# Cross-attention on one core: the fourth batch's x loaded one slot earlier, two query copies and the last products reordered, the first normalisation cut in halves

## The chip, the cores and the metric

The kernel runs on one core of a Trainium2 chip. A core has five engines with queues of their own: TensorE (PE, matmuls; PEld is its weight load), VectorE (DVE), ScalarE (ACT), GpSimd (POOL) and SyncE (SP), which here issues nearly all DMAs. Each engine takes its instructions in the order of the program, and they wait for each other by semaphores. The metric is the device time of one execution in microseconds: the median of several runs. Beside it stands one execution with the hardware profiler on.

## The reference

Eight batches of 256 tokens with 1024 columns attend to 256 context rows; 32 heads of 32 columns; everything is float32.

```python
residual = hidden_states                       # x, (8, 256, 1024)
x = (hidden_states - mu) * rsqrt(var + 1e-5) * ln_gamma + ln_beta
Q = _split_heads(x @ Wq.T)
K = _split_heads(memory_keys)                  # both are the context
V = _split_heads(memory_values)
scores = einsum('bhsd,bhtd->bhst', Q, K) * HEAD_DIM ** (-0.5)
scores = where(mask, scores, -inf)
probs = softmax(scores, axis=-1)
attn = einsum('bhst,bhtd->bhsd', probs, V)     # then heads side by side
return residual + attn @ Wout.T
```

## The kernel before

**Slots.** The work is cut into `N` = 64 slots, `n`, eight to a batch (`NQ` = 8). A slot stands for four heads (128 columns) of one batch. The loop at L903 writes the whole program out by hand; no scheduler reorders it. In slot `n` TensorE computes the scores of `n + 1` (`scores`, L471), the product of probabilities and values of `n - 2` (`values`, L614), query columns of later slots (`make_q`, L331, and from batch 3 `query_product`, L432), and a share of the output projection of the batch before (`product_steps`, L681). Queries and projection of most batches are done as 7 products of half-size blocks instead of 8, with sums of the weights and of the operands (names S1 to S4, T1 to T4, A11 to A22, B11 to B22); POOL makes these sums.

**Softmax.** `softmax_parts` (L491) of slot `n + 1` runs in slot `n`. For each of four heads: VectorE subtracts and takes a minimum (L515), ScalarE takes the exponential with its sum (L519), VectorE the reciprocal (L526), POOL scales (`normalize`, L528), and VectorE transposes in blocks of 32 (`blocks`, L534) into the tile `pT`. ScalarE copies half of it to `pc` (`aside`, L540). Two pairs of DMAs then exchange quarters between partitions: `pT<-pT` (L600) and, after the loads of the list `between`, `pT<-pc` (L604). Those four and `between` are the function `tail`; for softmaxes 1 to 7 it is kept back and run inside the next softmax, after its first head. Softmax 8 and most later ones run theirs at once.

**The places of the query copies.** ScalarE copies query products out of PSUM (`copy_q`, L344). In `softmax_parts` the list `copies` is run after the last exponential where `n <= NQ` (L572), and else after the third block transpose (L591), behind the first `aside`. Here `n` is the number of the softmax, one more than the slot.

**PSUM.** Four banks hold scores, two the values, one (`ps_q`, tile `pq`) queries, and one (`ps_o`) both the output products `po` and, in slots 1 to 8, a second query product: `make_q(..., second=True)`. In slot 8 this second product is finished and has to be copied before slot 9 starts the first output product (A11) in the same bank. `keep_p1` (L700) copies A11 out on ScalarE after six exponentials, before the product A12 goes on in that bank.

**x.** `load_x` (L125) brings a row block of 128 tokens (512 KB). Two tiles serve x and its transposed form `xe` in turn. For each batch a table gives the slots in which the two rows are loaded, their statistics taken (`ln_stats`, L216, on VectorE), normalised (`ln_norm`, L241), transposed (`blocks_x`, L307, VectorE) and moved by DMA (`move_x`, L327, `xnT<-xe`). For batch 3 (`SPLIT`) the rows are loaded in slots 6 and 7 (L801), and their statistics are taken in slots 8 and 9. In slots up to 8 the statistics are fillers (`fill`) between the steps of the softmax.

**Loads between.** The list `between` of slot `n` (L906 to L931) holds, in this order, keys or values, residual rows, x, mask and a table of output-weight halves (`load_wo`, L169, 512 KB each; L921). Batch 0's first residual row is loaded in slot 6 (L926).

**Start and end.** Before the loop batch 0's two rows are normalised on VectorE by one instruction each over 1024 columns (L853, L860), then transposed on TensorE; 32 transposes of the identity (L120) keep TensorE working before. After the loop the last batch's products are written out by hand (L1025 to L1084): `end_sum` makes the sums of one column block, `end_steps` adds products into PSUM, `end_add` adds PSUM to the residual. In the last slot ScalarE first runs the list `now`, a copy of a `po` bank to `ends` (`copy_po`, L707), then `copy_at` (L629), which copies the values to the tile `at`.

Of the kernel before, what the change touches and what calls it, by code (L numbers as in the profile page):

```python
# [59 lines left out]
def xattn_kernel(  # L60
# [11 lines left out]
    nc = tc.nc  # L72
    B, S, D = x.shape
# [3 lines left out]
    NQ = NC  # L77
# [9 lines left out]
    N = B * NQ  # L87
# [150 lines left out]
        else:  # L238
            later.append(pow_)

    def ln_norm(b, s, engine):  # L241
        if engine is nc.scalar:
            shift = sm.tile([P, 1], F32, tag="shift", name=f"shift_{b}_{s}", bufs=2)
            nc.gpsimd.tensor_scalar(
                shift, mvs[b][:, s, 0:1], rstds[b][:, s : s + 1], -1.0, ALU.mult, ALU.mult
            )
            engine.activation(
                xs[b][:, s, :], xs[b][:, s, :], AF.Identity,
                bias=shift, scale=rstds[b][:, s : s + 1],
            )  # L250
            return
        engine.tensor_scalar(
            xs[b][:, s, :], xs[b][:, s, :], mvs[b][:, s, 0:1], rstds[b][:, s : s + 1],
            ALU.subtract, ALU.mult,
        )

# [234 lines left out]
    def softmax_parts(n, copies=(), ahead=(), between=(), hooks={}, fill=()):  # L491

        fill = list(fill)

        def fill_in():
            if fill:  # L500
                fill.pop(0)()

        pss = scs[n]
        pT = pTs[n] = ptp.tile([P, 2, NI, NH, NS, K], F32, tag="pT", name=f"pT_{n}")
        pc = asp.tile([P, NI, NH, NS, K], F32, tag="pc", name=f"pc_{n}")
        es, mns, dens = {}, {}, {}

        def exps(j, part=range(NS)):
            if 0 in part:
                es[j] = ep.tile([P, NS, T], F32, tag="e", name=f"e_{n}_{j}")  # L510
                mns[j] = sm.tile([P, NS], F32, tag="mn", name=f"mn_{n}_{j}")
                dens[j] = sm.tile([P, NS], F32, tag="den", name=f"den_{n}_{j}")
            e, mn, den = es[j], mns[j], dens[j]
            for s in part:
                nc.vector.tensor_tensor_reduce(  # L515
                    out=e[:, s, :], in0=pss[j][:, s, :], in1=mbs[n // NQ], scale=1.0,
                    scalar=NO_SCORE, op0=ALU.add, op1=ALU.min, accum_out=mn[:, s : s + 1],
                )
                nc.scalar.activation(  # L519
                    e[:, s, :], e[:, s, :], AF.Exp, bias=mn[:, s : s + 1], scale=-1.0,  # L520
                    accum_out=den[:, s : s + 1],
                )

        def normalize(j):
            rden = sm.tile([P, NS], F32, tag="rden", name=f"rden_{n}_{j}")
            nc.vector.reciprocal(rden, dens[j])  # L526
            for s in range(NS):
                nc.gpsimd.tensor_scalar(  # L528
                    es[j][:, s, :], es[j][:, s, :], rden[:, s : s + 1], 1.0,
                    ALU.mult, ALU.mult,  # L530
                )

        def blocks(j):
            nc.vector.transpose(  # L534
                pT[:, :, :, j, :, :].rearrange("p a i s k -> p (a i) s k"),
                es[j].rearrange("p s (b t) -> p b s t", t=K),
            )

        def aside(j):
            nc.scalar.copy(pc[:, :, ts(j, 2)], pT[:, 1, :, ts(j, 2)])  # L540

        if n == 0:
            for j in range(NH - 1):
                exps(j, (0,))
            yield
            exps(NH - 1, (0,))
            fill_in()
            yield
            for j in range(NH):
                exps(j, (1,))  # L550
            normalize(0)
            fill_in()
        else:
            exps(0)
            while tails:
                tails.pop()()
            late = "p1" in hooks
            if not late:
                for done in list(pvs):
                    copy_at(done)  # L560
            exps(1)
            for hook in hooks.get("soon", ()):
                hook()
            exps(2)
            normalize(0)
            for hook in hooks.get("p1", ()):
                hook()
            exps(3)
            if late:
                for done in list(pvs):  # L570
                    copy_at(done)
        if n <= NQ:  # L572
            for copy in copies:
                copy()
        for hook in hooks.get(0, ()):
            hook()
        normalize(1)
        fill_in()
        blocks(0)
        for hook in hooks.get(1, ()):  # L580
            hook()
        normalize(2)
        fill_in()
        blocks(1)
        aside(0)
        normalize(3)
        fill_in()
        blocks(2)
        while fill:
            fill_in()  # L590
        if n > NQ:  # L591
            for copy in copies:
                copy()

        def tail():
            blocks(3)
            aside(1)

            for r in range(2):
                nc.sync.dma_start(pT[ts(2 * r, K), 1], pT[ts(2 * r + 1, K), 0])  # L600
            for load in between:
                load()
            for r in range(2):
                nc.sync.dma_start(pT[ts(2 * r + 1, K), 0], pc[ts(2 * r, K)])  # L604

        for load in ahead:
            load()
        if n < NQ or N - NQ < n < N - 1:
            tails.append(tail)
        else:  # L610
            tail()
        yield
# [145 lines left out]
    def end_steps(po, name, which, chunks, begins=(), cols=slice(0, 512)):  # L758

        for c in chunks:  # L760
            nc.tensor.matmul(  # L761
                po, end_operand(name)[:, c], wo[:, which, c, cols],
                start=c in begins, stop=True, skip_group_check=True,
            )
# [25 lines left out]
    for b in range(1, B):  # L790
        first = NQ * (b - 1) + 2
        if b == 1:
            when = dict(moves=())
        elif b == 2:
            when = dict(
                loads=(0, 1), stats=(2, 3), norms=(3, 3), trans=(4, 5),
                moves=tuple(5 + (i + 2) // 6 for i in range(16)),
            )
        else:
            when = dict(  # L800
                loads=(first - 12, first - 11) if b == SPLIT else (first - 13, first - 12),  # L801
                stats=(first - 10, first - 9) if b == SPLIT else (first - 11, first - 9),
                norms=(first - 8, first - 7), trans=(first - 7, first - 6),
                moves=tuple(first - 6 + (i + 2) // 6 for i in range(16)),
            )
        for table, key in (
            (loads, "loads"), (stats, "stats"), (norms, "norms"), (trans, "trans"),
        ):
            for i, n in enumerate(when.get(key, ())):
                assert n < first  # L810
                table[n].append((b, i))
        for n in range(N):
            part = [i for i, slot in enumerate(when["moves"]) if slot == n]
            if part:
                assert n < first - 1
                moves[n].append((b, part))
        biases[NQ * b - 2].append(b)
        if b % 2 == 0:
            masks[NQ * b - 7].append(b)
# [30 lines left out]

    ln_stats(0, 0)
    ln_stats(0, 1, (0,))
    ln_norm(0, 0, nc.vector)  # L853
    ln_stats(0, 1, (1, 2))
    transpose_x0(0)
    early, late = (0, 1, 5, 2, 6, 3), (7, 4)
    for c in early + late:
        copy_x0(0, c, nc.vector if c > 4 else nc.scalar)
    nc.gpsimd.tensor_copy(xnT0[:, :, S], bet)
    ln_norm(0, 1, nc.vector)  # L860
    first_q(0, early + late)
    mask_bias(0)
    transpose_x0(1)
# [39 lines left out]
    for n in range(N):  # L903
# [15 lines left out]
        between += [partial(load_x, *args) for args in loads[n]]  # L919
        between += [partial(load_mask, one) for one in masks[n]]  # L920
        for which, pair in {  # L921
            0: ((B12, 0),), 1: ((B22, 0),), 2: ((B11, 0), (B12, 1)), 3: ((B22, 1),),
            4: ((B11, 1), (B21, 0)), 5: ((B21, 1),),
        }.get(n, ()):
            between.append(partial(load_wo, which, pair))
        if n == NQ - 2:  # L926
            between.append(partial(load_res, 0, 0, 0))
        if n == N - 4:
            again = xp.tile([P, NS, D], F32, tag="x", name="x_again")
# [22 lines left out]
        if n in products:  # L952
            query_product(*products[n])
            copies.append(partial(copy_product, *products[n]))
        for one in now:
            one()
        fill = []
        if n < 2:
            transpose_x1(2 * n)
# [5 lines left out]
        if n + 1 < N:  # L965
            softmax(n + 1, copies, ahead, between, hooks, fill)
        else:
            copy_at(n - 2)
            for load in between:
                load()  # L970
        if b >= 0 and i == 1:
# [70 lines left out]
    )  # L1042
    end_steps(to_c11, "A12", B21, (0,), (0,))
    end_steps(to_c21, "A22", T4, (0,), (0,))
    end_steps(to_c22, "S1", T1, (0,), (0,))
    end_steps(to_c11, "A12", B21, (1,))
    end_steps(to_c21, "A22", T4, (1,))
    values(N - 2)
# [8 lines left out]
    copy_at(N - 1)  # L1057
    end_sum(slice(3, 4), nc.vector)
    first_cols, last_cols = slice(0, 384), slice(384, 512)
    end_steps(to_c22, "S1", T1, (1,))  # L1060
    end_steps(s2t2, "S2", T2, (2,))
    for r in (r01, r10, r11):
        end_add(r, s2t2)
# [61 lines left out]
```

## Time and profile before

| What | us |
|---|---|
| Median of 3 runs | 577.23 (575.44 to 579.26) |
| The profiled execution, device time | 577.06 |
| Its span, first to last instruction | 575.3 |
| TensorE busy | 567.5 (99%) |
| VectorE busy | 459.1 (80%) |
| ScalarE busy | 411.6 (72%) |
| GpSimd busy | 403.8 (70%) |
| DMA queue of SyncE, share of 16 engines | 68.8% |
| Bytes moved by DMA | 117.98 MB |

A busy TensorE is not TensorE at its peak: matmuls are pipelined and their ends are modelled. The mean granted clock was 0.997 of full speed. Times in timelines count from the start of the span. In a timeline row the columns are start, duration, engine, line, operation, tiles (out<-in), shapes, count, and in brackets the idle time of that engine before the row with what ended it. In a row by stretches the columns are the stretch, its length, then the busy time with the number of instructions in brackets for PE, PEld, DVE, ACT and POOL, the granted TensorE clock, the DMA share and GB/s. In a row of waits: who waited, for what, total us, times, longest.

### The profile page before, as it was taken

What the parts mean: (1) busy time and instruction counts of PE and PEld (TensorE: products, weight loads), DVE (VectorE), ACT (ScalarE), POOL (GpSimd) and SP (SyncE); (2) the same over time, 40 slices, a digit from 0 to 9 for tenths busy, and PEclk for the clock granted to TensorE, in tenths of its full rate; (3) what the DMA queues carried; (4) which work ended last, traced back from release to release, by engine and by line L of the source; (5) the groups of instructions that cost most, each with busy time, mean ns of one, the idle gap of its engine ahead of it and who ended that gap; (6) DMA issues with size and microseconds to landing.
All of it is one profiled execution on the core that took longest, in us unless ns stands there. A gap on an engine that the chain in (4) does not pass through costs nothing.

```text
span 575.3 us, 20001 instructions
## 1 busy us (share of the span) xinstructions
PE 567.5 (99%) x7162; PEld 393.2 (68%) x7162; DVE 459.1 (80%) x1696; ACT 411.6 (72%) x1424; POOL 403.8 (70%) x675
## 2 busy tenths in 40 slices
PE   8999998999999999999999999999999999999997
PEld 8778884667667777677676677667766767755444
DVE  5897986888877879889888888888877868879824
ACT  3697886677667867698667967778766876769820
POOL 1788896899896896766567675666657657448780
PEclk9999998999999999999999999999999999999999
DMA  8667877666778677877677776897568865536751
GB/s 303 233 191 234 236 223 200 203 194 187 191 235 270 202 199 194 252 227 222 182 230 230 214 204 195 241 272 203 144 182 267 241 196 138 140 107 180 205 163 74
DMA packets 47475, 117.98 MB, mean 205 GB/s; under 512 B 9104, under 2 KB 9872, under 8 KB 47376
## 3 DMA queue, kind: packets, MB, share of 16 engines
q1 hardware_dynamic: 47088, 116.69, 68.8%
q8 instruction: 57, 0.93, 0.7%
q14 instruction: 42, 0.34, 0.2%
q10 hardware_dynamic: 288, 0.01, 0.0%
HBM read 65.28 MB, written 11.53 MB: 134 GB/s over the span
## 4 chain that ended last, share of the span: by engine, by line
PE 84%; DMA 4%; POOL 4%; DVE 3%; ACT 2%; issue 1%; SPq 1%; DVEq 0%; ACTq 0%
PE po_S L694 20%; PE pq_A L440 16%; PE po_A L694 11%; PE pv L622 11%; PE sc L479 10%; PE pq L340 7%; PE pq_S L440 6%; PE po_end L761 2%; POOL e L528 2%; DMA wq<-in_wq_dram 2%; DMA x<-in_x_dram 1%; DVE e L515 1%; ACT e L519 1%; DVE pT L534 1%; PE po_last L761 1%
## 5 line engine op out<-in xcount | busy, mean ns | idle before, releaser
L528 POOL TENSOR_SCALAR e<-e,rden 128x256 f32<-128x256 f32 x512 | 235.7, 478 | 129.5 <-DVE rden L526 127.5
L519 ACT ACTIVATE e<-e,mn 128x256 f32<-128x256 f32 x512 | 254.0, 500 | 49.4 <-DVE mn L515 48.3
L534 DVE STREAM_TRANSPOSE pT<-e 128x512 f32<-128x512 f32 x256 | 180.7, 707 | 54.0 <-POOL e L528 34.8
L515 DVE CUSTOM_DVE_ANT_0 e<-sc,mb 128x256 f32<-128x256 f32 x512 | 186.0, 416 | 24.2 <-PE sc L479 23.6
L540 ACT COPY pc<-pT 128x512 f32<-128x512 f32 x128 | 79.0, 617 | 72.1 <-DVE pT L534 42.4
L519 ACT ACTIVATION_READ_ACCUMULATOR e<-e,mn 128x1 f32 x512 | 97.8, 191 | 0.0
L340 PE MATMUL pq<-xnT,wq 128*128 128x256 f32 (+1 forms) x368 | 84.1, 382 | 0.0
L340 PEld LDWEIGHTS pq<-xnT,wq 128*128 128x128 f32 x368 | 68.7, 190 | 14.3 <-issue 4.0
L479 PEld LDWEIGHTS sc<-k,qa 32*128 32x128 f32 x1024 | 46.1, 184 | 42.4 <-issue 22.0
L622 PE MATMUL pv<-pT,v 64*32 64x128 f32 x4096 | 74.5, 274 | 0.2
L622 PEld LDWEIGHTS pv<-pT,v 64*32 64x32 f32 x4096 | 57.0, 105 | 25.6 <-issue 11.6
L694 PE MATMUL po_S<-wo,at 128*128 128x512 f32 x152 | 74.3, 606 | 0.0
L479 PE MATMUL sc<-k,qa 32*128 32x256 f32 x1024 | 73.6, 400 | 0.1
L694 PE MATMUL po_A<-wo,at 128*128 128x512 f32 x128 | 62.4, 622 | 2.7 <-ACT qa L349 2.7
L694 PE MATMUL po_S<-wo,s 128*128 128x512 f32 x104 | 50.1, 605 | 0.0
L526 DVE RECIPROCAL rden<-den 128x2 f32<-128x2 f32 x256 | 37.7, 147 | 6.6 <-ACT e L519 5.3
L515 DVE DVE_READ_ACCUMULATOR2_ANT mn<- 128x1 f32 x512 | 42.7, 83 | 0.0
L694 PEld LDWEIGHTS po_A<-wo,at 128*128 128x128 f32 x128 | 23.2, 195 | 28.3 <-issue 23.2
L440 PEld LDWEIGHTS pq_A<-xnT,wq 128*128 128x128 f32 x320 | 37.3, 192 | 4.8 <-issue 4.1
L694 PEld LDWEIGHTS po_S<-wo,at 128*128 128x128 f32 x152 | 25.8, 190 | 19.8 <-issue 19.3
L440 PE MATMUL pq_A<-xnT,wq 128*128 128x128 f32 x320 | 37.3, 275 | 0.0
L635 ACT COPY at<-pv 128x128 f32<-128x128 f32 x128 | 26.1, 253 | 9.6 <-PE pv L622 9.6
(95 smaller groups left out, 605.9 us busy)
## 6 DMA issues: line engine op xcount, KB each, us to landing
v<-in_kv_dram SPq DMA_DIRECT2D x32, 512.0 KB, 4.6
pT<-pT SPq DMA_DIRECT2D x128, 128.0 KB, 2.9
pT<-pc SPq DMA_DIRECT2D x128, 128.0 KB, 4.1
ring<-kept_T SPq DMA_DIRECT2D x18, 512.0 KB, 5.3
k<-in_kv_dram SPq DMA_DIRECT2D x32, 256.0 KB, 4.2
x<-in_x_dram SPq DMA_DIRECT2D x14, 512.0 KB, 5.6
r<-in_x_dram SPq DMA_DIRECT2D x28, 256.0 KB, 4.7
out_dram<-r SPq DMA_DIRECT2D x28, 256.0 KB, 3.4
```

The source lines that it names most:

```text
L340: nc.tensor.matmul(pqs[n], wq[:, o, c, :], xnTs[b](c), start=(c == 0), stop=(c == NC - 1),)
L440: nc.tensor.matmul(pqs[b][:, o, :], w[:, c], x_[:, c], start=begins and o + c == 0, stop=c == NK - 1, skip_group_check=True,)
L479: nc.tensor.matmul(scs[n][j][:, s, :], qa[r, n % NQ, ts(s, P)], ks[n - n % 2][r, n % 2, :], start=True, stop=True,)
L515: nc.vector.tensor_tensor_reduce(out=e[:, s, :], in0=pss[j][:, s, :], in1=mbs[n // NQ], scale=1.0, scalar=NO_SCORE, op0=ALU.add, op1=ALU.m ...
L519: nc.scalar.activation(e[:, s, :], e[:, s, :], AF.Exp, bias=mn[:, s : s + 1], scale=-1.0, accum_out=den[:, s : s + 1],)
L526: nc.vector.reciprocal(rden, dens[j])
L528: nc.gpsimd.tensor_scalar(es[j][:, s, :], es[j][:, s, :], rden[:, s : s + 1], 1.0, ALU.mult, ALU.mult,)
L534: nc.vector.transpose(pT[:, :, :, j, :, :].rearrange("p a i s k -> p (a i) s k"), es[j].rearrange("p s (b t) -> p b s t", t=K),)
L540: nc.scalar.copy(pc[:, :, ts(j, 2)], pT[:, 1, :, ts(j, 2)])
L622: nc.tensor.matmul(pvs[n][r][j * HD : (j + 1) * HD], vs[n - n % 2][ts(r, 2 * K), i, ds(n % 2 * P + j * HD, HD)], pT[ts(r, 2 * K), :, i, j, ...
L635: nc.scalar.copy(ats[b, k][:, c, :, ts(r, 2), :], pv.rearrange("p a s k -> p s a k"))
L694: nc.tensor.matmul(po, operand(b, name)[:, c], wo[:, which, c], start=begins and c == 0, stop=c == NK - 1, skip_group_check=not begins,)
```

## The change

There are five edits.

1. Batch 3's rows of x are loaded in slots 5 and 6 rather than 6 and 7. The second pairs of output weights B12 and B22 move from slots 2 and 3 to slots 3 and 4, B21's pairs from 4 and 5 to 5 and 6, and the first residual row from slot 6 to slot 7.
2. In softmax 9 (slot 8) the first query copy is run after the last exponential; the second stays late. All other softmaxes keep their places.
3. Batch 0's rows are each normalised by two instructions of 512 columns.
4. In the last slot `now` runs after `copy_at` rather than before.
5. In the end the first S1 product is no longer issued after the first A12 and A22 products; it is issued with the second S1 product, after `values(N - 1)`.

No instruction is added beyond those of edit 3. Apart from one matmul, one copy in slot 8, one copy in the last slot and the loads named, every engine has its instructions in the order it had before.

```diff
-    def ln_norm(b, s, engine):
+    def ln_norm(b, s, engine, cols=slice(0, D)):
...
-            xs[b][:, s, :], xs[b][:, s, :], mvs[b][:, s, 0:1], rstds[b][:, s : s + 1],
+            xs[b][:, s, cols], xs[b][:, s, cols], mvs[b][:, s, 0:1], rstds[b][:, s : s + 1],
...
-        if n <= NQ:
-            for copy in copies:
-                copy()
+        copies = list(copies)
+        for copy in copies[: NQ if n <= NQ else 1 if n == NQ + 1 else 0]:
+            copies.remove(copy)
+            copy()
...
-        if n > NQ:
-            for copy in copies:
-                copy()
+        for copy in copies:
+            copy()
...
-                loads=(first - 12, first - 11) if b == SPLIT else (first - 13, first - 12),
+                loads=(first - 13, first - 12),
...
-    ln_norm(0, 0, nc.vector)
+    for h in range(2):
+        ln_norm(0, 0, nc.vector, ts(h, 512))
...
-    ln_norm(0, 1, nc.vector)
+    for h in range(2):
+        ln_norm(0, 1, nc.vector, ts(h, 512))
...
-            0: ((B12, 0),), 1: ((B22, 0),), 2: ((B11, 0), (B12, 1)), 3: ((B22, 1),),
-            4: ((B11, 1), (B21, 0)), 5: ((B21, 1),),
+            0: ((B12, 0),), 1: ((B22, 0),), 2: ((B11, 0),), 3: ((B12, 1),),
+            4: ((B22, 1), (B11, 1)), 5: ((B21, 0),), 6: ((B21, 1),),
...
-        if n == NQ - 2:
+        if n == NQ - 1:
             between.append(partial(load_res, 0, 0, 0))
...
-        for one in now:
-            one()
+        if n + 1 < N:
+            for one in now:
+                one()
...
             copy_at(n - 2)
+            for one in now:
+                one()
...
-    end_steps(to_c22, "S1", T1, (0,), (0,))
...
-    end_steps(to_c22, "S1", T1, (1,))
+    end_steps(to_c22, "S1", T1, range(2), (0,))
```

## The prediction

> **What bounds the kernel now.** I read the page's table of engines first, then the waits, then the timeline of the one stretch the waits point at. The profiled execution took 577.06 us (median of the runs 577.23 us; span 575.3 us, so 1.8 us lie around it).
>
> ```profile
> PE 567.5 (99%) x7162; PEld 393.2 (68%) x7162; DVE 459.1 (80%) x1696; ACT 411.6 (72%) x1424; POOL 403.8 (70%) x675
> ```
>
> TensorE is busy 567.5 of 575.3 us; the next engine has 80%. The end is TensorE's work plus TensorE's holes, and the change leaves its work alone (one matmul moves). The holes sum to 7.8 us. At the two ends 1.35 us pass before the first matmul and about 2.9 us after the last. Inside, the waits name three, two of them interior:
>
> ```profile
> PE po_A L694 <- ACT qa L349: 2.7, 1, 2.7
> PE busy L120 <- POOL ring masks.py:199: 1.3, 1, 1.3
> PE po_end L761 <- POOL ring L753: 0.4, 1, 0.4
> ```
>
> The 2.7 us hole seen by stretches of 4 us, and TensorE, ScalarE and VectorE around it in the timeline:
>
> ```profile
> 84.00:88.00 4.00, 4.00 (x20) 3.51 (x20) 2.38 (x14) 4.00 (x17) 3.49 (x6) 1.00 0.90 298
> 88.00:92.00 4.00, 2.03 (x21) 1.22 (x19) 2.83 (x9) 0.52 (x3) 1.11 (x3) 1.00 1.03 269
> 92.00:96.00 4.00, 3.24 (x4) 1.51 (x5) 3.85 (x19) 3.54 (x12) 4.00 (x6) 0.57 0.59 163
> ```
>
> ```profile
> 88.88 1.15 PE L479 MATMUL sc<-k,qa 32*128 32x256 f32 x16
> 89.13 0.69 DVE L226 BATCH_NORM_STATS2 st<-x 128x6 f32<-128x512 f32 x1 [2.66 <-DMA x<-in_x_dram]
> 91.72 0.62 ACT L540 COPY pc<-pT 128x512 f32<-128x512 f32 x1 [3.48 <-DVE rden L526]
> 92.24 0.83 ACT L349 ACTIVATE qa<-pq,qa 128x256 f32<-128x256 f32 x2
> 92.76 5.26 PE L694 MATMUL po_A<-wo,at 128*128 128x512 f32 x8 [2.73 <-ACT qa L349]
> ```
>
> This is slot 8 going into slot 9. VectorE's queue stands 2.66 us at the statistics of the fourth batch's first row of x, whose load lands at 89.1; the block transposes behind it are late, ScalarE's copy `pc` waits for them, the query copies stand behind `pc`, and the first output product needs the `po` bank that the first query copy empties. After the hole the granted clock is 0.57 over 92 to 96, and eight matmuls that take 3.63 us elsewhere (the chain of waits has `po_A x8` at 3.63 in every later batch) take 5.26: another 1.63 us. The hole costs 2.73 + 1.63 = 4.36 us.
>
> Here a rule speaks differently. The Trainium skill ("TensorE: Matmul & The Clock Gate", HAM oscillation) says that idle gaps over about 3.4 us bring the slow clock. By that rule the 2.73 us hole would cost 2.73 alone; the row shows the clock falling behind it, so I take 4.36. The same page calls the window free-running, so in some executions the 1.63 may be absent; the lowest run, 575.44, is 1.8 under the median, which fits but proves nothing.
>
> **The early query copy.** In slot 8 the first copy moves from behind `pc` to directly behind the last exponential, which ends at 88.23. It takes about 0.46 us (one of the pair that took 0.83), so the bank is free at about 88.7; TensorE asks for it when the scores end, at 88.88 + 1.08 = 89.96. Margin 1.3 us: hole gone. It was the same ACTIVATE, so no cost; it moves `pc` back 0.46 us into ScalarE's 3.48 us idle.
>
> **x of the fourth batch one slot earlier.** Its first row is issued near 74.6 instead of 83.46, nearly 9 us earlier, so the statistics at 86.47 find it and VectorE's queue comes forward 2.66 us. This is needed too. With the copy alone, the next thing on ScalarE would be late: `keep_p1` (L702) stands behind six exponentials of slot 9's softmax, started 94.06 in the trace, and must empty `po` before the second product writes it.
>
> **What is late next.** Without a hole slot 9 runs from 88.88: scores 1.08, first product 3.45 (eight matmuls at 0.43), values 1.09, so the second product asks at 94.5. The exponentials start 2.66 us earlier, at 91.4; six at 0.494 end at 94.4, `keep_p1` takes 0.59: 95.0. New wait about 0.5 us (0 to 1.0).
>
> The other late candidates are SyncE's. Its tail of slot 6 issued, before, values, weights and then the two `pT<-pc` moves (75.71, landing 4.6 us later at 80.35, the second some 0.3 later). Now one 512 KB row of x stands ahead of them. The issue itself (0.45 us) is hidden, since at 75.04 SyncE stood waiting till 75.65 for a landing. The transfer is not: two 512 KB loads issued at 65.60 and 66.09 landed 5.3 and 7.3 us later, that is 70.9 and 73.4, 2.5 us apart. The skill ("DMA: Bandwidth & Descriptors", Where 436 GB/s comes from) gives 435 GB/s as the ceiling, an estimate of 1.2 us for 512 KB; by it the moves land at 81.9 and nobody waits. The row gives up to 83.1. I take 2.0, near the row: 82.65 for the second. The values of slot 8 need them at 82.41: about 0.25 us late (none to 0.7).
>
> Behind that, the moves of slot 6 (`xnT<-xe`) and the next `pT` transfers slide. Slot 7's tail has weights (512 KB) where the residual row (256 KB) was: its issue slides 1.0 us, its `pT<-pc` from landing 91.1 (84.48 + 6.6) and about 91.8 to about 93.5 (92.7 to 94.1), wanted at 93.4. The next pair waits at issue for the `pT<-pT` that landed at 93.25 (86.32 + 6.9); 2 us more makes it land about 98.4, wanted at 98.3. The last six `xnT<-xe` follow: the last was issued 97.88 and landed 2.0 later; 2.05 more, less 0.65 because its first one's long issue should shorten, gives 101.3. The batch-2 queries that read it began at 104.93, so now 104.93 - 4.36 = 100.6: 0.7 us late (none to 2.0).
>
> These four waits are not added: a delay of TensorE at one satisfies the next. The largest decides: I take 0.7 us, range 0 to 2.0. A stop of that size is well under the 2.73 us that brought the slow clock, so nothing for the clock. Past slot 11 transfers have slack again: the values of slot 11 come at 111.34 - 4.36 = 107; their moves, issued at 100.92 and landing at the page's median 4.1 us later, were down by 105.1.
>
> **Moves that I cost at nothing, with their cover.** The weights B12, B22 (second pairs) come one slot later, but POOL's sums use them first at 84.39, and they land by 71 (the slot that B11 had). B21's first pair lands near 82, its second near 92.5, for a product that starts at 94.5 and uses the second pair with its third step, at about 96.2: cover about 4 us, the thinnest; each us over it would be a us of TensorE. The residual row lands near 97 and is stored with batch 0 after 104. Slot 2's tail loses one 512 KB load, which can only help.
>
> **Halves of columns.** TENSOR_SCALAR over 1024 took 0.803 us; two over 512 cost between 0 and 0.2 more (STREAM_TRANSPOSE takes 1.207 at 1024 and 0.707 at 512 columns, a fixed part of 0.2). Neither end reaches TensorE: in the trace the first transposes of x start at 7.72, when the warm-up matmuls end (7.89), though x was ready at 6.92; those of the second row follow the first query product without a hole. Gain or loss between -0.4 (another phase of the warm-up) and +0.1; I take 0.
>
> **The end.** One `S1` matmul no longer stands where TensorE waited for POOL:
>
> ```profile
> 548.73 0.58 ACT L712 COPY ends<-po_S 128x512 f32<-128x512 f32 x1
> 549.21 0.43 ACT L635 COPY at<-pv 128x128 f32<-128x128 f32 x2
> 549.77 1.12 PE L761 MATMUL po_end<-wo,ring 128*128 128x512 f32 x2 [0.43 <-POOL ring L753]
> ```
>
> Now the next matmuls need the `at` copies, which move ahead of `ends`: ready at 549.16 instead of 549.64. TensorE goes on at about 549.25: 0.5 us saved (0.3 to 0.55). `ends` is ready by 549.75, before POOL asks for it at 550.10; the values of the next slot start 1.3 us earlier, at 551.2, and their transfers landed about 550.1 to 550.5. The S1 chunks stand later at no extra work.
>
> **Sum.** 577.06 - 4.36 - 0.5 + 0.7 = 572.9 us; against the median 577.23 that is 573.1. I say 573.0, 0.7% less. About 1% (5.8 us) is what a measurement of this kernel can tell from no change, so even all of it, 4.9 us, stays within.
>
> **Rivals.** (1) The hole mostly moves, 16%: the transfers behind the extra row are down 2 to 4.4 us late, or `keep_p1` is. For: the DMA share is 0.90 and 1.03 in the two stretches from 84 to 92, and landings took up to 8.5 us there (the load at 87.58). Against: the row is the only extra before 82, and later 256 KB. At 3 us of stop the end comes to 575.2, with some slow clock 576.5. (2) More than summed, 8%: no new wait, the halves give 0.4 and the before's slow clock was more frequent than I think: 571.5 or a little less. (3) Slower, 4%: one mechanism, the last `xnT<-xe` move. If SyncE's issue queue holds it until it lands after 105.5, TensorE stops 4.9 us at the batch-2 queries in slot 10, all is given back, and a slow clock adds 1.7 (half of a window of about 3.4): 578.5; above 583 it must land after 109. Its measured issue to landing is 2.0 us, so SyncE would have to be 6 us late; I work out 1.4. That the change does nothing would need another reader of the bank; the copy waits for TensorE alone, so 1% or less, inside (1).
>
> The forecast proper, 572 to 574.5, holds 72%. Range 571.7 to 576.0: it takes in most of (1), leaves out (2), (3). Faster by over 1%: 8%; within 1%: 88%; slower by over 1%: 4%.
>
> **What the changed profile would show.** No `po_A` wait for `qa` near 90, clock 1.00 in 92 to 96, no wait of the statistics for x; the second product starting about 8 us after slot 9 begins with at most 0.7 us of TensorE holes in `pv`, `po_A` or `pq` between 82 and 102; no `po_end` wait for POOL. I am wrong if a hole over 2 us stands at a `pT`, `xnT` or B21 landing there, or if the clock falls again.

## The result and the profile after

The forecast gain did not come. The changed kernel takes 576.15 us (median of 12 runs, 574.67 to 577.84), the kernel before on the same chip 576.79 us (12 runs, 574.10 to 579.26). The ratio over the rounds is 0.9998, with a 95% interval of 0.9979 to 1.0016: no difference. Forecast were 573.0 us and a range of 571.7 to 576.0; the time lies just outside it, where rival (1) put it (575.2 to 576.5).

The profiled execution of after took 575.24 us (span 573.5), 1.8 us less than that of before. Its table of engines shows the same work on TensorE:

```profile
PE 565.9 (99%) x7162; PEld 392.1 (68%) x7162; DVE 459.2 (80%) x1698; ACT 412.3 (72%) x1424; POOL 403.8 (70%) x675
```

TensorE's waits in after (who, for what, total us, times, longest):

```profile
PE pq L340 <- DMA xnT<-xe: 2.1, 1, 2.1
PE busy L120 <- POOL ring masks.py:199: 1.3, 1, 1.3
PE pv L622 <- issue: 0.8, 2, 0.6
```

The waits of `po_A` for `qa` and of `po_end` for POOL are gone, as intended. In their place stand 2.1 us at the batch-2 queries of slot 10, for the last `xnT<-xe` transfer, and 0.8 us at the values of slot 8. TensorE in the timeline of after:

```profile
80.87 1.15 PE L479 MATMUL sc<-k,qa 32*128 32x256 f32 x16
82.58 0.38 PE L622 MATMUL pv<-pT,v 64*32 64x128 f32 x2 [0.57 <-issue]
83.24 1.13 PE L622 MATMUL pv<-pT,v 64*32 64x128 f32 x62 [0.28 <-issue]
84.30 5.45 PE L340 MATMUL pq<-xnT,wq 128*128 128x256 f32 x24
89.68 1.15 PE L479 MATMUL sc<-k,qa 32*128 32x256 f32 x16
90.75 3.70 PE L694 MATMUL po_A<-wo,at 128*128 128x512 f32 x8
94.38 1.16 PE L622 MATMUL pv<-pT,v 64*32 64x128 f32 x64
95.47 2.84 PE L694 MATMUL po_A<-wo,at 128*128 128x512 f32 x6
98.24 1.15 PE L479 MATMUL sc<-k,qa 32*128 32x256 f32 x16
...
103.70 2.61 PE L340 MATMUL pq<-xnT,wq 128*128 128x256 f32 x11 [2.11 <-DMA xnT<-xe]
```

The first output product follows the scores at 90.75 without a hole and takes 3.70 us where it took 5.26; the second follows at 95.47. Two holes before it (0.57 and 0.28) and one behind it (2.11) sum to 2.96 us of idle time. They cost more than that: the first two matmuls of the values, cut off by the holes, take 0.38 us alone, where all 64 in one run take 1.16, because they overlap. A slot begins with its scores, so its length from scores to scores holds everything (us):

| Slot | before | after | after less before |
|---|---|---|---|
| 8, the values wait in after | 7.54 | 8.81 | +1.27 |
| 9, the hole of before | 12.93 | 8.56 | -4.37 |
| 10, the queries wait in after | 8.39 | 10.80 | +2.41 |

By stretches of 4 us (columns as before the prediction) the clock stays full where it was 0.57, and TensorE is short of work at 80 to 84 and at 100 to 104:

```profile
80.00:84.00 4.00, 3.15 (x78) 2.13 (x83) 3.51 (x13) 2.87 (x10) 3.98 (x7) 1.00 0.71 197
88.00:92.00 4.00, 4.00 (x28) 2.59 (x27) 3.27 (x13) 2.49 (x7) 3.69 (x6) 1.00 1.00 291
92.00:96.00 4.00, 4.00 (x71) 1.95 (x70) 2.14 (x13) 3.94 (x16) 3.58 (x6) 1.00 0.73 205
100.00:104.00 4.00, 1.89 (x36) 0.86 (x20) 3.93 (x20) 2.85 (x13) 3.21 (x4) 1.00 0.46 105
```

Why the last transfer is issued late is read from SyncE's queue. Its timeline in before:

```profile
74.59 0.45 SPq L173 DMA_DIRECT2D wo<-in_woT_dram  x1
75.71 1.15 SPq L604 DMA_DIRECT2D pT<-pc  x2
76.91 4.62 SPq L327 DMA_DIRECT2D xnT<-xe  x6
...
94.05 4.42 SPq L327 DMA_DIRECT2D xnT<-xe  x6
```

and in after:

```profile
74.53 0.44 SPq L130 DMA_DIRECT2D x<-in_x_dram  x1
75.02 0.43 SPq L173 DMA_DIRECT2D wo<-in_woT_dram  x1
75.55 1.15 SPq L604 DMA_DIRECT2D pT<-pc  x2
76.75 5.95 SPq L327 DMA_DIRECT2D xnT<-xe  x6
82.81 1.59 SPq L600 DMA_DIRECT2D pT<-pT  x2
...
94.61 1.95 SPq L604 DMA_DIRECT2D pT<-pc  x2
96.61 3.75 SPq L327 DMA_DIRECT2D xnT<-xe  x6
```

The row of x at 74.53 is new. The six moves behind it take 5.95 us to issue instead of 4.62, because SyncE has to wait at the sixth (its own waits between 73 and 104):

```profile
SPq L327 <- DMA wo<-in_woT_dram: 2.2, 1, 2.2
```

From there everything on SyncE is late: the next group of six starts at 96.61 instead of 94.05. The chain of waits of after carries it to TensorE:

```profile
87.33 7.26 DMA pT<-pT
...
95.22 1.34 SPq L604
...
99.77 3.69 DMA xnT<-xe
103.46 0.24 issue
103.70 2.40 PE pq L340 x10
```

The last move was issued at 99.77 and landed 3.69 us later; in before it was issued at 97.88 and landed 2.0 us later. The queue was not full here: the DMA share is 0.46 from 100 to 104, and the five moves issued just ahead of the last one landed 2.0 us after their issue, like the last five in before. What was late is one part. A DMA reports its landing in sixteen parts, each counted in its semaphore. Fifteen parts of the last move were in at 101.81, 2.04 us after the issue; the sixteenth came at 103.46. In between the trace has one packet of 16 KB of another queue, which loads instructions (100.88 to 102.41), and the last data packets of the move begin at 102.40, when it ends. In e12 below, the same kernel once more, it is the same: fifteen parts at 102.13, a 16 KB packet from 101.22 to 102.50, the last part at 103.73. That this packet held the part up is read from these times; no experiment moves it. Without the late part TensorE would have waited about 0.5 us here, by an estimate (landing at 101.81, plus the 0.24 us of the chain, less 101.59, when its matmuls before ended).

At the end edit 5 does what it should; TensorE has no hole there any more:

```profile
546.12 3.83 PE L761 MATMUL po_end<-wo,at 128*128 128x512 f32 x8
```

From the scores of the last slot to the end of the span before took 35.65 us and after 35.07: 0.58 us less. The account of the two profiled executions: 0.58 us at the end; 0.69 us in slots 8 to 10, by the table above; and 0.46 us at the start, where the warm-up matmuls took 6.08 instead of 6.54 us and the first transposes of x begin at 7.26 rather than 7.72 (not the halves: in e1 and e2 below, which don't have them, they begin at 6.99 and 7.16). That is 1.73 of the 1.8 us.

### The profile page after: what moved, and what is told of

Its sections match the earlier page's. It is cut to its first block, busy times and chain, and to the rows that moved or that the text cites. A ratio compares the mean times of both kernels' runs of the same rounds, so it can differ in the third digit from the quotient of the medians.

```text
span 573.5 us, 20000 instructions
## 1 busy us (share of the span) xinstructions
PE 565.9 (99%) x7162; PEld 392.1 (68%) x7162; DVE 459.2 (80%) x1698; ACT 412.3 (72%) x1424; POOL 403.8 (70%) x675
## 4 chain that ended last, share of the span: by engine, by line
PE 86%; POOL 4%; DVE 4%; DMA 2%; ACT 1%; issue 1%; SPq 1%; DVEq 0%; ACTq 0%; POOLq 0%
PE po_S L694 20%; PE pq_A L440 16%; PE pv L622 11%; PE sc L479 10%; PE po_A L694 10%; PE pq L340 7%; PE pq_S L440 6%; PE po_end L761 3%; POOL e L528 3%; DVE e L515 2%; DMA pT<-pT 1%; PE po_last L761 1%; ACT e L519 1%; PE busy L120 1%; DVE pT L534 1%
## 5 line engine op out<-in xcount | busy, mean ns | idle before, releaser
L519 ACT ACTIVATE e<-e,mn 128x256 f32<-128x256 f32 x512 | 254.1, 501 | 51.2 <-DVE mn L515 50.8
L519 ACT ACTIVATION_READ_ACCUMULATOR e<-e,mn 128x1 f32 x512 | 97.9, 191 | 0.0
L694 PE MATMUL po_A<-wo,at 128*128 128x512 f32 x128 | 60.9, 609 | 0.0
```

Source lines behind the costliest of these rows:

```text
L519: nc.scalar.activation(e[:, s, :], e[:, s, :], AF.Exp, bias=mn[:, s : s + 1], scale=-1.0, accum_out=den[:, s : s + 1],)
L694: nc.tensor.matmul(po, operand(b, name)[:, c], wo[:, which, c], start=begins and c == 0, stop=c == NK - 1, skip_group_check=not begins,)
```

## Experiments

**Theory (T):** the edits remove the holes as worked out, but the loads that edit 1 moves put 768 KB more in front of the small transfers of slots 6 to 8 (in slot 5 the row of x, in slot 6 weights of 512 KB where the residual row had 256), and TensorE waits for those transfers instead. **Rivals:** that the hole between slots 8 and 9 was worth much less than 4.36 us, so there was little to gain; that the early copy or another edit costs time; that something other than loads would be late next whatever was done. Where several kernels ran on one chip, they share the runs of the kernel before: 577.19 us there for the first group (e1, e2, e4, e5), 575.64 for the second (e6 to e9), 577.59 for the third (e10 to e12).

### Edit 2 alone (e1_copy)

Before with only this:

```diff
-        if n <= NQ:
-            for copy in copies:
-                copy()
+        copies = list(copies)
+        for copy in copies[: NQ if n <= NQ else 1 if n == NQ + 1 else 0]:
+            copies.remove(copy)
+            copy()
```

> The kernel before with the early query copy alone (edit 2). Theory T (the gain went into transfers that the moved x row pushed back): the transfers stay those of before, the last xnT<-xe is down near 100.4, and no wait for it shows. But VectorE still waits 2.7 us for x, so the wait of po_A for qa goes and the second product waits for keep_p1 instead: about 3.2 us of TensorE idle near 94.5 to 97.7; time 575.9, or 577.5 where the slow clock follows. Rival R (a hole taken from slot 8 is given back at xnT<-xe whatever is loaded): idle before pq of 1.5 us or more at a landing of xnT<-xe after 102.

Measured: 577.8 us, ratio 1.0013 (0.9983 to 1.0043). TensorE's longest wait, and the row in its timeline:

```profile
PE po_A L694 <- ACT p L702: 2.3, 1, 2.3
```

```profile
96.44 4.25 PE L694 MATMUL po_A<-wo,at 128*128 128x512 f32 x6 [2.34 <-ACT p L702]
```

The copy frees the bank, and the same delay of VectorE's queue reaches TensorE one product later, at `keep_p1`. Alone it is worth nothing. The six matmuls took 4.25 us instead of 2.84, at a granted clock of 0.71 from 96 to 100.

### Edit 1 alone (e2_loads)

Before with only the table of loads (x in slots 5 and 6, the weights, the residual row).

> The kernel before with the moved loads alone (edit 1). Theory T: VectorE does not wait for x, the copy pc comes near 89.0 and the first query copy behind it near 89.6 to 90.0, so po_A loses at most 0.5 us even without the early copy; but the wait of pq for xnT<-xe of 2 us or more stands as in the changed kernel, its landing past 102.5. Time as the changed kernel's, 575.5 to 576.5. Rival C (the early copy is what counts): po_A still waits over 1.5 us for qa, time 577 or more.

Measured: 577.42 us, ratio 0.9992 (0.9967 to 1.0018). TensorE's timeline:

```profile
84.70 2.38 PE L622 MATMUL pv<-pT,v 64*32 64x128 f32 x64 [2.59 <-ACT e L519]
```

The hole at `po_A` is gone without the early copy, and a hole of 2.59 us, with the clock at 0.57 from 84 to 88, stands at the values of slot 8. I had not expected it there, and the expected wait at the queries is absent. The exponential named ended at 84.50, but it belongs to a later softmax: what these values need and what came last is the first `pT<-pc` behind the moved loads, down at 84.61 (the weights issued ahead of it at 75.94 landed at 84.04, and SyncE stood from 81.14 to 84.06 for them). The place differs from after, the cause is the same queue.

### Old loads, statistics one slot later (e4_late_stats)

Edits 2 to 5, the loads as before; instead of an earlier load, a later reader:

```diff
-                stats=(first - 10, first - 9) if b == SPLIT else (first - 11, first - 9),
+                stats=(first - 9, first - 8) if b == SPLIT else (first - 11, first - 9),
```

> The changed kernel with the loads of before (x in slots 6 and 7, weights and row where they were), and the statistics of batch 3 taken in slots 9 and 10 rather than 8 and 9, so that VectorE need not wait for x. Theory T: no bytes more than before ahead of the transfers, so the last xnT<-xe is down by about 100.5 and TensorE's idle between 78 and 106 sums to less than 1 us; time 572 to 573, ratio 0.991 to 0.994. Rival R (given back whatever is loaded): a wait of 1.5 us or more at xnT<-xe or pT, time 575 to 577.

Measured: 572.14 us, ratio 0.9923 (0.9895 to 0.9952). All that TensorE waits for:

```profile
PE busy L120 <- POOL ring masks.py:199: 1.3, 1, 1.3
PE pq L340 <- DMA xnT<-xe: 0.2, 1, 0.2
```

Its profiled execution took 572.22 us, 4.84 less than that of before; the prediction's two gains sum to 4.86. Slot 9 takes 8.56 us where before took 12.93. So the hole was worth what was worked out, and the rival that it was worth little falls. The view of the twelve moves issued between 74 and 104 us (durations of the issues, and their time to landing, which it knows for seven of the twelve in before, five in after and three here) sets the three kernels side by side; before:

```profile
L327 SPq DMA_DIRECT2D xnT<-xe x12: 582/590/1442, 76.9 to 97.9; - x12
DMA to landing us min/median/max: 2.0/3.8/4.7
```

after:

```profile
L327 SPq DMA_DIRECT2D xnT<-xe x12: 507/590/607, 76.7 to 99.8; - x12
DMA to landing us min/median/max: 2.0/6.5/7.3
```

and e4_late_stats:

```profile
L327 SPq DMA_DIRECT2D xnT<-xe x12: 581/592/1552, 77.3 to 98.3; - x12
DMA to landing us min/median/max: 2.8/3.5/3.9
```

The moves of 64 KB are the same in all three. Only in after do moves take over 6 us: by the counts of their semaphores the first five of slot 6 took 5.9 to 7.8 us there, 3.4 to 4.7 in before and 3.0 to 4.8 here.

### After without two of the weight loads (e5_no_b21)

```diff
+    B21 = B22
...
-            4: ((B22, 1), (B11, 1)), 5: ((B21, 0),), 6: ((B21, 1),),
+            4: ((B22, 1), (B11, 1)),
```

> The changed kernel without the loads of the weight block B21 (two of 512 KB, in slots 5 and 6); B22 is used in its place, so the output is not the reference's. Theory T, by bytes: 1 MB less stands ahead of slot 7's xnT<-xe, 512 KB less ahead of the pT<-pc of slot 6. The wait of pq for xnT<-xe falls from 2.1 us to below 0.5, idle between 78 and 106 below 1 us, time 572.5 to 573.5. Rival O (SyncE's order and its waits at issue set the landing, not the bytes): the wait stays at 1.5 us or more, time within 1 us of the changed kernel's.

Measured: 572.32 us, ratio 0.9919 (0.9888 to 0.9949). The only wait inside is this (lines stand one lower in this kernel):

```profile
PE po_A L695 <- ACT p L703: 0.2, 1, 0.2
```

This kernel leaves out B21, so its output is not the reference's; the amount of work is the same. The row of x stays in slot 5; with two loads, 1 MB, fewer on the queue in slots 5 and 6 the full gain is there. So it is what the queue carries. Whether the bytes count or the number of loads does this run can't tell, since SyncE has two issues fewer too.

### The late statistics alone (e7_stats_alone)

Before with the one line of e4.

> The kernel before with one line changed: the statistics of batch 3 in slots 9 and 10 rather than 8 and 9, no early copy. If the wait of VectorE for x is the whole root of the first hole (theory W), pc comes near 88.3 and the first query copy behind it ends near 89.3, before the scores end at 89.6: no wait of po_A over 0.3 us, idle of TensorE between 78 and 106 below 1 us, time 572.5 to 573.5. If the place of the copy matters by itself (rival C), po_A waits 0.7 us or more and the time is 573.5 to 575.

Measured: 573.3 us, ratio 0.9955 (0.9937 to 0.9972). In its profile TensorE is busy 4.00 of 4.00 us in each stretch from 80 to 104. It stands 0.9 us just before, at the values of slot 7 (76.25), and this execution, 574.62, is the slowest of the twenty. One changed line gives most of what can be had: the median is 1.2 us above that of e4, though not on one chip.

### The late statistics on top of after (e8_after_late_stats)

After with the same line; from e4 it differs in the loads alone.

> The changed kernel with its own loads (x in slots 5 and 6, weights and row later), and the statistics of batch 3 in slots 9 and 10. Against e4_late_stats only the loads differ. Theory T (the moved loads put the transfers back): idle of 1.5 us or more at values of slot 8 or 9 or at pq for xnT<-xe, time 575 to 577.5. Rival S (the statistics in slot 8 were the harm, the loads none): idle below 1 us, time 572 to 573.

Measured: 576.05 us, ratio 1.0001 (0.9976 to 1.0025). TensorE's timeline:

```profile
81.04 1.15 PE L479 MATMUL sc<-k,qa 32*128 32x256 f32 x16
84.86 2.33 PE L622 MATMUL pv<-pT,v 64*32 64x128 f32 x64 [2.67 <-ACT e L519]
87.12 6.08 PE L340 MATMUL pq<-xnT,wq 128*128 128x256 f32 x24
```

The hole of e2 is back, at the same place, and the clock falls to 0.63 from 84 to 88. The loads of e4 and those of after, everything else alike, are 3.9 us apart (572.14 and 576.05, though not on one chip).

### Weights moved, x not (e9_weights_late)

e4 with the weights and the residual row where the change puts them, x still in slots 6 and 7:

```diff
-            0: ((B12, 0),), 1: ((B22, 0),), 2: ((B11, 0), (B12, 1)), 3: ((B22, 1),),
-            4: ((B11, 1), (B21, 0)), 5: ((B21, 1),),
+            0: ((B12, 0),), 1: ((B22, 0),), 2: ((B11, 0),), 3: ((B12, 1),),
+            4: ((B22, 1), (B11, 1)), 5: ((B21, 0),), 6: ((B21, 1),),
...
-        if n == NQ - 2:
+        if n == NQ - 1:
```

> e4_late_stats with the weights and the first residual row moved as in the change, x left in slots 6 and 7. Slot 5 then loads no more than before, slots 6 and 7 each 256 KB more. If the x row in slot 5 is what counts (theory X), values of slot 8 do not wait, and the last xnT<-xe slides by at most 1 to 1.5 us: time 572 to 573.5. If the weights in slots 5 to 7 count (rival B), the wait for xnT<-xe or for pT is 1.5 us or more, time 574.5 to 577.

Measured: 574.06 us, ratio 0.9973 (0.9953 to 0.9993). TensorE's timeline:

```profile
98.94 1.47 PE L622 MATMUL pv<-pT,v 64*32 64x128 f32 x64 [1.06 <-DMA pT<-pc]
```

About half of the loss, and between what the two theories expected: e8, on the same chip, has the rows of x a slot earlier besides and takes 2.0 us more. So both kinds of load cost time.

### After with the last moves issued first (e6_moves_first)

After, with the six `xnT<-xe` of slot 7 put into `between`, ahead of softmax 8's `pT<-pc`:

```diff
+            between += [partial(move_x, *args) for args in moves[n]]
...
-        for args in moves[n]:
+        for args in moves[n] if n != NQ - 1 else ():
```

> The changed kernel with slot 7's six xnT<-xe issued before the pT<-pc of softmax 8 rather than behind it, so that they do not stand behind SyncE's wait of about 4.9 us for the pT<-pT. Theory Q (in-order issue on SyncE is a part of the landing at 103.5): the last xnT<-xe is down near 98.5 to 100, the wait of pq goes, and 0.3 to 1.0 us come back at the values of slot 10, whose pT<-pc is issued 1 to 2 us later; time 573.5 to 575. Rival B (bytes alone set it): the wait stays, at pq or at pT, at 1.5 us or more, time as the changed kernel's, 575 to 577.

Measured: 574.6 us, ratio 0.9977 (0.9952 to 1.0002), not clearly faster than before. The wait at the queries is gone, and `pv` waits instead, four times in slots 8 and 10 (a longer wait of 1.5 us stands at the start, for the first query weights):

```profile
PE pv L622 <- issue: 0.5, 2, 0.3
PE pv L622 <- ACT pc L540: 0.4, 1, 0.4
PE pv L622 <- DMA pT<-pc: 0.3, 1, 0.3
```

The order on the queue chooses who is late; 1.2 us of holes stay there, less than in after.

### Without the early copy (e10_no_early_copy)

e4 without edit 2:

```diff
-        for copy in copies[: NQ if n <= NQ else 1 if n == NQ + 1 else 0]:
+        for copy in copies[: NQ if n <= NQ else 0]:
```

> e4_late_stats without the early query copy (both copies of slot 8 behind the third block transpose again). Theory W (VectorE's wait for x was the whole root; with it gone the copy comes in time at either place): no wait of po_A over 0.3 us, time within 0.5 us of e4_late_stats on the same chip. Rival C: po_A waits 0.5 us or more, time 0.7 us or more above.

Measured: 572.43 us, ratio 0.991 (0.9877 to 0.9944), with no wait of TensorE inside at all. Both copies are done when the product asks (ScalarE's timeline):

```profile
88.93 0.83 ACT L349 ACTIVATE qa<-pq,qa 128x256 f32<-128x256 f32 x2
```

Once VectorE doesn't stand, the early copy is not needed; nor does it cost anything.

### e4 and after once more, on one chip (e11_late_stats_again, e12_after_again)

> The kernel of e4_late_stats again, beside the changed kernel on one chip. Theory T: ratio to the kernel before 0.990 to 0.995, and 3 to 4 us under the changed kernel, with a narrower spread of its runs. If the first verdict was luck: ratio 0.997 or more.

> The changed kernel again, beside the others on one chip. Theory T: ratio to the kernel before 0.997 to 1.002 as at first, and a hole of TensorE of 2 us or more at values of slot 8 or at pq in slot 10; where it stands in slot 8 the last xnT<-xe is waited for no longer.

Measured: 572.61 us, ratio 0.9921 (0.9898 to 0.9943) for e11; 576.66 us, ratio 0.9986 (0.9966 to 1.0006) for e12. The two are 4.05 us apart, and differ only in the loads and the slots of the statistics. In e11's profile slots 8 to 10 take 7.54, 8.57 and 8.39 us: nothing is lost there. Its runs do not lie closer together than those of e12, as I had expected (571.59 to 577.83 against 574.15 to 578.82): two of them had a mean clock of 0.997. In e12's profile the wait of after is there again, and the clock falls behind it (stretch 104 to 108); its two longest waits inside, and its stretch:

```profile
PE pq L340 <- DMA xnT<-xe: 2.4, 1, 2.4
PE pv L622 <- issue: 0.6, 2, 0.4
```

```profile
104.00:108.00 4.00, 4.00 (x12) 3.22 (x13) 2.95 (x9) 2.06 (x7) 4.00 (x10) 0.60 0.83 205
```

e4 and its repeat are the version that beats both kernels: about 0.8% faster than before.

## Why the prediction was wrong, step by step

- **The hole of 4.36 us and its removal: right.** From scores to scores slot 9 is 4.37 us shorter in after. Without a hole in its place (e4, e11) the medians fall by 5.05 and 4.98 us against before on the same chips: 4.36 and 0.58 from the end make 4.94. That the agreement is so close is in part luck, since the medians of before also hold executions with more and with less of the slow clock.
- **The early copy: right as a step, and rightly called insufficient alone.** The wait at `keep_p1` (e1) was worked out; there it took 2.3 us. That the copy is not needed beside the other part (e10) I had not seen.
- **x one slot earlier: right for VectorE.** The statistics wait for nothing in after.
- **What is late next: the step that failed.** The prediction put the new wait at 0.7 us, 0 to 2.0, at the last `xnT<-xe`. The place was right, the size not: the queries there cost 2.11 us of idle time, and the values of slot 8 0.85 before them (I had 0.25, at most 0.7), 2.96 in all, or 3.68 counted from scores to scores. A slow clock comes on top in part of the executions; in medians it all makes 4.05 us (e12 less e11). Three terms were too small.
  - First, the price of the 512 KB row. The second `pT<-pc` took 6.99 us to land, at 83.15, where before's took 4.4. That is the trace's own 2.5 us between two such loads, which I had cut to 2.0. The 1.2 us that I estimated from the Trainium skill ("DMA: Bandwidth & Descriptors", Where 436 GB/s comes from) took that page's ceiling; for loads from HBM, as this one is, the same place says that a lower limit of about 358 GB/s binds, by an estimate 1.5 us. The measured 2.5 decides against both.
  - Second, the issue of the row, costed at nothing because SyncE stood there anyway. The stand came later instead, 2.2 us at the sixth move, so the last move was issued at 99.77 rather than 99.28.
  - Third and largest, the last move's landing: 103.46 where I had 101.3. The 2.0 us of flight held for fifteen of its sixteen parts; the last part came 1.65 us behind them, at the packet that loads instructions. The prediction has no such term. Without it the wait at the queries would have been about 0.5 us, by the estimate above, well within the predicted range.
- **"These four waits are not added": wrong in part.** The values put TensorE 1.27 us back, and the queries still waited 2.11 us, because the last move was later than that could cover.
- **"Nothing for the clock": wrong.** It followed from the wait's size. In after's twelve runs seven show a mean clock of 0.996 or 0.997, in e12 ten of 21, and e12's profile shows the fall right behind its hole of 2.38 us.
- **`keep_p1` 0.5 us:** hardly there. In after TensorE came later itself, at 95.47; in e4 and e11, where nothing delays it, no wait shows either, and e5 has 0.18.
- **Moves costed at nothing:** the products never waited for the moved weights, so the cover of each held. What was left out is what these loads do to the queue: e9 has 1.06 us of hole from them and the residual row.
- **The halves: right** (none seen at TensorE; 0.99 us for two against 0.81 for one, hidden). **The end: right**, 0.58 for 0.5.
- **The sum** with the measured terms: 577.06 - 4.37 - 0.58 - 0.46 (the start) + 3.68 = 575.3, against 575.24 profiled. The failure lies in one term of the sum. Rival (1), "the hole mostly moves", is what happened. The argument against it ("the row is the only extra before 82") overlooked that small transfers behind one 512 KB load are each late by it, and that a move which is late can meet something else that it missed before.

Not tried: the row of x moved with the weights left, the weights taken to another place with x in slots 5 and 6, and the load of instructions moved. How the 4 us split between the row and the weights is known from e9 and e8 alone.

## What to carry to other kernels

When a reader stands for a load that comes late, ask first whether the reader can be moved: here one line that takes the statistics a slot later gave what the earlier load, with five others shuffled around it, did not. A bulk load put earlier on a shared queue is paid by the small transfers behind it; price their flight from rows where the queue is full. A transfer is there only with its last part: where a margin is down to tenths of a us, look at the slowest part in the trace, not at the usual flight. If removing a hole changes nothing, list the waits of the changed kernel before doubting the hole.

## What the runs showed of the hardware

- **Half clock behind short holes, in part of the executions.** Single holes of 2.34 to 2.73 us had granted clocks of 0.57 to 0.71 in the stretch behind them (before, e1, e2, e8, e12); the hole of 2.11 in after's profile had none. The Trainium skill ("TensorE: Matmul & The Clock Gate", HAM oscillation) speaks of gaps over about 3.4 us. The clock records of the five traces show more: each slow time lasts 3.41 us at half clock, and begins a whole number (23 to 29) of 3.41 us after the clock first rose. In the 3.41 us ahead of it TensorE had stood for 2.1 (e1) to 2.7 us (e8). In after such an edge (101.81) cut the hole into 0.2 and 1.9 us, and the clock stayed. So where a hole falls counts beside its length, as far as these six traces show.
- **How often the half clock comes differs.** Of 46 runs of before in the third group 15 have a mean clock of 0.999 or more (mean 575.24 us), 21 one of 0.996 or 0.997 (578.17 us) and 10 one of 0.993 or 0.994 (580.03 us). On the chip of the second group 39 of 55 kept 0.999 or more (575.11 us), which accounts for most of the 2 us by which the median of before is lower there. The medians of kernels with next to no hole inside agree on two chips (572.14 and 572.32; 572.43 and 572.61). All eight runs of e5 kept 0.999 or more and lie within 0.73 us; those of before spread over 8.6 us beside them.
- **A transfer lands in sixteen parts, and one late part holds its reader.** In after and e12 the last move's sixteenth part came 1.65 and 1.60 us behind the fifteenth, and its packets began when a 16 KB packet of instructions ended. In e4 the packet begins at 99.95; all parts of the last move were in at 100.32, and the two `pT<-pT` behind it had the late part instead (1.37 and 1.11 us). A late part does not need such a packet: of the row of x for which VectorE stood in before, fifteen parts were in at 87.36 and the last at 89.11, with no load of instructions between. What held that one up stays open.
- **An issue on SyncE can stand for a load long before it.** The sixth move in after started when the weights issued at 75.02 had landed, at 82.19; in before an issue at 73.41 started when a load of weights landed, at 73.39. In the trace each of these pairs has one semaphore: SyncE's DMAs in this program take eight semaphores in turn, and an issue waits here for the eighth before it. So this is the program's use of semaphores, and no limit of the queue is shown.
- **The name behind a wait misled twice.** e2's and e8's holes are put down to the exponentials of ScalarE (`e L519`). The first `pT<-pc` landed 0.09 us before TensorE went on in both (84.61 and 84.77), and the holes vanish with the loads.
